# Eleven filter groups beside each image's scans in place of eight, and the stages ahead of them dealt more densely

## The chip, the cores and the metric

The kernel runs on one core of a Trainium2 chip. The metric is the device time of one execution in microseconds. Three runs of the kernel before took 11284.48, 11290.91 and 11290.32 us, a median of 11290.32. The profile is one further execution, of 11279.9 us.

## The reference

Four images of 64 x 64 positions with 128 channels pass through two layers, in 32-bit floats. What matters here:

```
# layer 0: four selective scans over 4096 positions (by rows, by columns, and both backwards),
# 256 channels, 16 states each
h = exp(dt * A) * h + (dt * u) * B          # one step per position
y = sum over the states of h * C
x = x + out_proj(norm(sum of the four y) * silu(z))
# then a mixture of 64 experts: softmax over positions, the top 8 of each expert,
# two matrices with a gelu between, scattered back and added to x
# layer 1: three matrices over x and its row and column sums, added to x, then on t = norm(x):
U_plus, U_minus = convolution of t with 16 long filters (4096 taps), plain and with alternating signs
out = sum over filters of U_plus @ Mpp[k] + U_minus @ Mpm[k]     # and three short taps
x = x + out
```

The long convolutions are computed as a block transform: positions go to 64 slots of a short Fourier transform, short filters are applied there, and the result is turned back.

## The kernel before, in words

**The scans.** The four images are worked on one after the other. An image's scans are four directions of eight chunks of 512 positions, 32 chunks, and each chunk has 16 steps, one for each state, 2048 steps in all. Both halves of 256 channels (128 partitions each) are in one step:

- SP loads the step's B and C, broadcast over partitions (`bc`), five steps ahead.
- ACT takes the exponential `da` (L1365), three steps ahead.
- DVE multiplies `db = du * B` (L1392, 128x1024) and runs two scans (L1398, 128x512) into `hh`, which has five buffers.
- POOL keeps the last state (L1407) and multiplies by C (L1408), one step later.
- PE sums over states by transposing `hh` into `y` (L1434), two steps later.

For every next chunk the step sizes are made meanwhile, a piece for each step: PE projects them (`dt_ps`, L1280), ACT and POOL make a softplus of them (`dl`, `dx`, L1282 to L1299), and ACT copies `dx` to PSUM as `du` at the chunk's end (`into_psum`, L1346), once the last `db` has been read.

**The work beside the scans.** Everything else is written as Python generators that issue a piece of work and yield its weight. `beside(b)` strings them together for the image whose scans are running: beside the first image the stages ahead of the other images' scans, beside image b the stages behind the scans of image b - 1. These are `after_scans` (the four `y` of an image are read back as `yk`, summed, normalised, gated and projected, L485 to L575), `experts_and_sums` (norms, logits, softmax, top 8, the two expert matrices `w1t` and `w2t` of 16 MB each, and layer 1's matrices) and `to_slots` (the transform, `fu_ps`, L1052). Then come groups of filters, `convolve`. Image 3's slot also turns image 0's results back (`from_slots`, `gi_ps`), and the first of these slots has one more gate.

`deal` is called twice in a step. It adds a share of the slot's total to what is due, and takes pieces until what has been made reaches it:

```
share["due"] += WEIGHT[chunks[i][0]] / ((K * NSC - FIRST) * (N - len(BUSY)) * 2)
while share["made"] < share["due"]:
    share["made"] += next(share["pieces"], 1e9)
    tick()
```

It deals nothing in an image's first chunk nor at the second and third step of any chunk. Each dealt instruction is pinned behind the scan's last instruction on its engine, and the next transpose of `y` behind the last dealt matmul, so the order on PE is the written one. Whatever is left at an image's end is run at once.

**A group of filters.** There are 64, sixteen an image, each over four slots of the transform. A group has four parts, in which 16 matmuls `cv_ps` (L1116) apply short filters and are evicted to `y` (L240, L238), and two accumulations of 16 matmuls `zq_ps` (L1137) with the matrices `me` and `mo`; the sum is transposed (`zt_ps`) and stored. Beside the scans a `cv_ps` pair weighs 4.0, a `zq_ps` matmul 2.0 and an eviction of `zq_ps` 4.0. There, PSUM leaves a single two-bank slot for `cv_ps`, `zq_ps` and the scans' own `dt_ps`. The trace counts two records for one of these 32-bit matmuls; transposes have one.

**The tail.** The groups that no scan covers follow the last scan, with eight banks of PSUM, evictions shared by ACT and DVE, and weights 4.0 for a `zq_ps` and 0 for `cv_ps`. A first loop runs the last image's three stages and deals filters between its pieces: for each unit of stage, `ratio` units of filters. A second one does the same with the turning back of images 1 and 2 and the last sixteen groups. At last image 3 is turned back.

Of the kernel before, what the change touches and what calls it, by code (L numbers as in the profile page):

```python
# [1 line left out]

# [1 line left out]

# [14 lines left out]
B, H, W, C = 4, 64, 64, 128  # L19
# [12 lines left out]


FIRST = 1
WEIGHT = (1346.0, 2087.0, 2005.0, 2059.0)

BUSY = (2, 3)

LAG = 5.0

BESIDE = 8


BS = 32
# [34 lines left out]
def kernel(  # L79
# [138 lines left out]
    def bank(shape, name):  # L218

        if side["ones"]:  # L220
            return side["ones"].tile(shape, F32, name=name, tag="ps")
        n = int(np.prod(shape[1:]))
        ap = pair(name)[0 : shape[0], 0, 0:n]
        if len(shape) == 2:
            return ap
        sizes = {f"d{i}": d for i, d in enumerate(shape[1:])}
        names = " ".join(sizes)
        return ap.rearrange(f"p ({names}) -> p {names}", **sizes)
# [5 lines left out]
    def evict(dst, src):  # L234

        side["n"] = side.get("n", 0) + 1
        if side["tail"] and side["n"] % 2:
            nc.vector.tensor_copy(dst, src)  # L238
        else:
            nc.scalar.copy(dst, src)  # L240
# [21 lines left out]
    def pipelined(n, *stages):  # L262


        for step in range(n + len(stages) - 1):
            for s in reversed(range(len(stages))):
                if 0 <= step - s < n and stages[s]:
                    stages[s][1](step - s)
                    yield stages[s][0]
# [49 lines left out]
    def sigmoid_of(pool, ps, h):  # L319


        n = ps.shape[-1]
        e = pool.tile([P, n], F32, name="sg_e")
        v = pool.tile([P, n], F32, name="sg_v", bufs=3)
        if h is None:
            nc.scalar.activation(e, ps, AF.Exp, scale=-1.0)
            nc.scalar.copy(v, ps)
        else:
            nc.scalar.activation(e, ps, AF.Exp, scale=-1.0, bias=ncb[:, h : h + 1])
            nc.scalar.activation(v, ps, AF.Identity, bias=cb[:, h : h + 1])  # L330
        nc.scalar.activation(e, e, AF.Ln, bias=1.0)
        nc.scalar.activation(e, e, AF.Exp, scale=-1.0)
        return v, e
# [121 lines left out]
    def gate(b):  # L455

        z_d[b] = dram.tile([2, P, L], F32, name=f"z_d{b}")
        with tc.tile_pool(name="pa_z", bufs=2) as pz:
            xn, vs = {}, {}

            def load(i):
                if i % 2 == 0:
                    g = i // 2
                    xn[g] = pz.tile([P, 512], F32, name="xn_z", bufs=4)
                    nc.sync.dma_start(xn[g], xn_d[b][:, 512 * g : 512 * (g + 1)])

            def project(i):
                g, h = divmod(i, 2)
                ps = bank([P, 512], "zp")
                nc.tensor.matmul(  # L470
                    ps, w_in_t[:, DI + h * P : DI + (h + 1) * P], xn[g], start=True, stop=True
                )
                vs[i] = sigmoid_of(pz, ps, None)

            def mul(i):
                v, s = vs[i]
                nc.gpsimd.tensor_mul(v, v, s)

            def put(i):
                g, h = divmod(i, 2)  # L480
                nc.sync.dma_start(z_d[b][h, :, 512 * g : 512 * (g + 1)], vs[i][0])

            yield from pipelined(16, (0.5, load), None, None, (2.8, project), (1.3, mul), (0.5, put))
# [551 lines left out]
    def to_slots(b):  # L1035

        with tc.tile_pool(name="fu", bufs=3) as fp:
            ub, uo = {}, {}

            def load(g):  # L1040

                ub[g] = fp.tile([NB, 4, 2, C], F32, name="ub")
                nc.sync.dma_start(
                    ub[g].rearrange("j t a c -> j (t a) c"),
                    u_d[b].rearrange("(j t) c -> j t c", j=NB)[:, 8 * g : 8 * g + 8, :],
                )

            def turn(g):
                uo[g] = fp.tile([P, 4, 2, C], F32, name="uo")
                for a in range(2):  # L1050
                    ps = bank([P, 4, C], "fu_ps")
                    nc.tensor.matmul(ps, fu_t, ub[g][:, :, a, :], start=True, stop=True)  # L1052
                    evict(uo[g][:, :, a, :], ps)

            def put(g):
                for r in range(2):
                    nc.sync.dma_start(
                        ud[b][:, r, 4 * g : 4 * g + 4], uo[g][r * NQ : (r + 1) * NQ]
                    )

            yield from pipelined(BS // 4, (0.5, load), (2.0, turn), (1.0, put))
# [122 lines left out]
    def from_slots(b):  # L1184

        with tc.tile_pool(name="gi", bufs=3) as gp:
            zb, xr, iv = {}, {}, {}

            def here(g):
                t0 = 2 * (BS - 4 * (g + 1))  # L1190
                return slice(t0, t0 + 8)

            def load(g):
                zb[g] = gp.tile([P, 4, 2, C], F32, name="zb")
                for r in range(2):
                    nc.sync.dma_start(
                        zb[g][r * NQ : (r + 1) * NQ], zd[b][:, r, 4 * g : 4 * g + 4]
                    )

            def turn(g):  # L1200
                xr[g] = gp.tile([NB, 4, 2, C], F32, name="xr3", bufs=4)
                nc.sync.dma_start(
                    xr[g].rearrange("j t a c -> j (t a) c"),
                    x3_d[b].rearrange("(j t) c -> j t c", j=NB)[:, here(g), :],
                )
                iv[g] = gp.tile([NB, 4, 2, C], F32, name="iv")
                for a in range(2):
                    ps = bank([NB, 4, C], "gi_ps")
                    nc.tensor.matmul(ps, gi_t, zb[g][:, :, a, :], start=True, stop=True)  # L1209
                    nc.scalar.activation(iv[g][:, :, a, :], ps, AF.Identity, scale=wpj[0:NB, :])  # L1210

            def add(g):

                for t in range(4):
                    nc.gpsimd.tensor_add(xr[g][:, t], xr[g][:, t], iv[g][:, 3 - t])  # L1215

            def put(g):
                nc.sync.dma_start(
                    out[b].rearrange("(j t) c -> j t c", j=NB)[:, here(g), :],
                    xr[g].rearrange("j t a c -> j (t a) c"),  # L1220
                )

            yield from pipelined(BS // 4, (0.7, load), (2.5, turn), (3.0, add), (0.5, put))
# [6 lines left out]
    all_groups = [(b, G) for b in range(B) for G in range(NQ // 4)]  # L1230

    def beside(b):

        if b == 0:
            for i in range(1, B):
                yield from before_scans(i)
            for i in range(B - 1):
                yield from gate(i)
            yield from filters()
        else:  # L1240
            yield from after_scans(b - 1)
            yield from experts_and_sums(b - 1)
            yield from to_slots(b - 1)
            if b == 1:
                yield from gate(B - 1)
            if b == B - 1:
                yield from from_slots(0)
            yield from convolve(all_groups[BESIDE * (b - 1) : BESIDE * b])

    with ExitStack() as c0:  # L1250
# [65 lines left out]
        def deal(*behind):  # L1316
# [4 lines left out]
            start = len(traced)  # L1321
            share["due"] += WEIGHT[chunks[i][0]] / ((K * NSC - FIRST) * (N - len(BUSY)) * 2)
            while share["made"] < share["due"]:
# [24 lines left out]
        for s in range(-5, total + 2):  # L1348
# [23 lines left out]
            if 0 <= s < total:  # L1372
                b, k, step, _ = chunks[i]
# [29 lines left out]
            if 0 <= t < total:  # L1403
                _, tk, tstep, _ = chunks[t // N]
                if tstep < NSC - 1:
                    last = 0 if tk >= 2 else SC - 1
# [63 lines left out]
    def first_stages():  # L1470
        yield from after_scans(B - 1)
        yield from experts_and_sums(B - 1)
        yield from to_slots(B - 1)
# [5 lines left out]
    last = len(all_groups) - NQ // 4  # L1479
    with tc.tile_pool(name="cv_tail", bufs=2) as cp:  # L1480

        for stages, groups, ratio in (
            (first_stages(), all_groups[BESIDE * (B - 1) : last], 3.2),
            (back(), all_groups[last:], 18.0),
        ):
            filtered = convolve(groups, cp)
            due = made = 0.0
            start = len(traced)
            for weight in stages:
                tick()  # L1490
                behind(start, False)
                start = len(traced)
                due += weight * ratio
                while made < due:
                    made += next(filtered, 1e9)
                    tick()
                behind(start, True)
                start = len(traced)
            run(filtered)
            behind(start, True)  # L1500
# [76 lines left out]
```

## Time and profile before

| | |
|---|---|
| median of three runs | 11290.32 us |
| the profiled execution | 11279.9 us |
| its span | 11278.1 us |
| scans of images 0, 1, 2, 3 start at | 301, 2437, 4633, 6876 us |
| last scan ends, first tail loop ends | 9088, about 10490 us |
| busy over the span: PE, DVE, ACT, POOL | 75%, 72%, 55%, 64% |
| POOL `hh` (L1408), one | 2359 ns, 2048 of them |
| DVE scan (L1398) and `db` (L1392), one | 1267 and 1232 ns |
| granted TensorE clock: scans of image 1, tail | 0.80, 0.99 to 0.98 |

A group's row has the line, engine, operation, and output from inputs, then its busy time, the mean of one, and the idle time just before it with what ended it. In the table by stretch each engine has its busy time and instructions in that stretch, then the granted clock, the share of time in which the DMA engines were busy, and GB/s. A row of waits names who waited for whom, the total in us, the number of waits and the longest. "Slot" below means the time of one image's scans; chunks are counted from 0 within it.

### The profile page before, as it was taken

What the parts mean: (1) busy time and instruction counts of PE and PEld (TensorE: products, weight loads), DVE (VectorE), ACT (ScalarE), POOL (GpSimd) and SP (SyncE); (2) the same over time, 40 slices, a digit from 0 to 9 for tenths busy, and PEclk for the clock granted to TensorE, in tenths of its full rate; (3) what the DMA queues carried; (4) which work ended last, traced back from release to release, by engine and by line L of the source; (5) the groups of instructions that cost most, each with busy time, mean ns of one, the idle gap of its engine ahead of it and who ended that gap; (6) DMA issues with size and microseconds to landing.
All of it is one profiled execution on the core that took longest, in us unless ns stands there. A gap on an engine that the chain in (4) does not pass through costs nothing. (4 is left out here: it accounts for less than half of the span.)

```text
span 11278.1 us, 117105 instructions
## 1 busy us (share of the span) xinstructions
PE 8435.7 (75%) x34656; PEld 4819.2 (43%) x34656; DVE 8146.8 (72%) x7046; ACT 6181.0 (55%) x12043; POOL 7262.7 (64%) x6518
## 2 busy tenths in 40 slices
PE   6677676556776777757766777576677789999998
PEld 2444443334453444444543344455344444355443
DVE  0898888887987999879878898798698932222222
ACT  4757575657466565664655566657455544124222
POOL 1888787888787877787867788888687821001001
PEclk9687787757777888878778788787788899999999
DMA  2565656566655666657565566575666664553555
GB/s 97 164 202 186 203 170 202 192 188 201 226 178 178 197 180 193 204 163 249 166 174 167 167 192 207 167 264 155 171 198 181 183 163 122 151 137 95 140 131 120
DMA packets 901457, 1980.14 MB, mean 176 GB/s; under 512 B 101562, under 2 KB 415578, under 8 KB 899290
## 3 DMA queue, kind: packets, MB, share of 16 engines
q1 hardware_dynamic: 900826, 1972.65, 58.2%
q8 instruction: 283, 4.64, 0.2%
q14 instruction: 348, 2.85, 0.1%
HBM read 1766.77 MB, written 205.52 MB: 175 GB/s over the span
## 5 line engine op out<-in xcount | busy, mean ns | idle before, releaser
L1408 POOL TENSOR_TENSOR hh<-hh,bc 128x1024 f32<-128x1024 f32 x2048 | 4829.8, 2359 | 434.2 <-DVE hh L1398 192.2
L1398 DVE TENSOR_TENSOR_SCAN hh<-da,hst,db 128x512 f32<-128x512 f32 x3584 | 4392.9, 1267 | 675.6 <-PE y L1434 297.9
L1365 ACT ACTIVATE da<-dl,aneg 128x512 f32<-128x512 f32 x4096 | 2766.3, 716 | 2084.4 <-DVE hh L1398 1998.3
L1434 PE MATMUL y<-ident,hh 128*128 128x128 f32 x16384 | 2808.2, 322 | 1214.8 <-POOL hh L1408 1095.7
L1434 PEld LDWEIGHTS y<-ident,hh 128*128 128x128 f32 x16384 | 2293.9, 167 | 2637.0 <-POOL hh L1408 1424.9
L1392 DVE TENSOR_TENSOR db<-du,bc 128x1024 f32<-128x1024 f32 x2048 | 2523.5, 1232 | 633.6 <-ACT du L1346 547.7
L1116 PE MATMUL cv_ps<-slab,us 64*128 64x512 f32 x4096 | 1197.3, 691 | 533.5 <-ACT y L240 277.8
L240 ACT COPY y<-cv_ps 128x512 f32<-128x512 f32 (+1 forms) x1024 | 754.3, 741 | 667.8 <-PE cv_ps L1116 638.0
L1407 POOL COPY hst<-hh 128x2 f32<-128x2 f32 x1792 | 338.9, 189 | 1123.6 <-DVE hh L1398 980.0
L1137 PE MATMUL zq_ps<-y,me 128*128 128x512 f32 x2048 | 1000.1, 609 | 49.0 <-ACT y L240 43.3
L1137 PE MATMUL zq_ps<-y,mo 128*128 128x512 f32 x2048 | 969.3, 597 | 0.0
L238 DVE COPY y<-cv_ps 128x512 f32<-128x512 f32 x640 | 441.5, 691 | 561.9 <-PE cv_ps L1116 511.8
L1116 PEld LDWEIGHTS cv_ps<-slab,us 64*128 64x128 f32 x4096 | 407.7, 206 | 1002.5 <-ACT y L240 369.3
L1153 POOL TENSOR_TENSOR zt<-zt,zt 128x512 f32<-128x512 f32 x64 | 81.2, 1268 | 996.2 <-DVE zt L238 536.5
L1398 DVE TENSOR_TENSOR_SCAN hh<-da,db 128x512 f32<-128x512 f32 x512 | 597.1, 1208 | 113.4 <-PE y L1434 70.8
L388 PE MATMUL cv_ps<-xh,diag 128*128 128x512 f32 x1152 | 534.7, 607 | 0.3 <-ACT xh L381 0.2
L1137 PEld LDWEIGHTS zq_ps<-y,me 128*128 128x128 f32 x2048 | 352.5, 193 | 382.2 <-issue 262.1
L1280 PE MATMUL dt_ps<-dts,dtw 8*128 8x512 f32 x512 | 371.4, 822 | 175.5 <-ACT dl L1283 48.3
L1137 PEld LDWEIGHTS zq_ps<-y,mo 128*128 128x128 f32 x2048 | 356.3, 191 | 316.6 <-issue 313.9
L1292 POOL TENSOR_TENSOR ex<-ex,dx 128x1024 f32<-128x1024 f32 x128 | 302.6, 2364 | 169.2 <-ACT dx L1289 169.0
L238 DVE COPY zt<-zq_ps 128x512 f32<-128x512 f32 x39 | 26.9, 691 | 529.0 <-PE zq_ps L1137 523.3
L510 PE MATMUL yk_ps<-yk,ident 128*128 128x512 f32 x512 | 275.2, 677 | 85.3 <-DMA yk<-y_d 34.0
(222 smaller groups left out, 8705.0 us busy)
## 6 DMA issues: line engine op xcount, KB each, us to landing
bc<-bc_d SPq DMA_DIRECT2D x2048, 512.0 KB
slab<-hd SPq DMA_DIRECT2D x1024, 256.0 KB
xc<-xc_d SPq DMA_DIRECT2D x128, 512.0 KB
y_d<-ys SPq DMA_DIRECT2D x128, 512.0 KB
w1t<-in_w_dram SPq DMA_DIRECT2D x128, 512.0 KB
w2t<-in_w_dram SPq DMA_DIRECT2D x256, 256.0 KB
xc_x<-xc_d SPq DMA_DIRECT2D x64, 512.0 KB
yk<-y_d SPq DMA_DIRECT2D x128, 256.0 KB
```

The costliest lines, as they stand in the source:

```text
L238: nc.vector.tensor_copy(dst, src)
L240: nc.scalar.copy(dst, src)
L388: nc.tensor.matmul(ps, diag[:, h, t, :], xh[:, 8 * g + dy : 8 * g + dy + 8, dx : dx + W], start=(t == 0), stop=(t == 8),)
L1116: nc.tensor.matmul(pq[q].rearrange("p (r k t) -> p r k t", r=2, t=BS), us[b, G][rows, p, a if e == 0 else 1 - a, :], slab[i][rows, p, :, : ...
L1137: nc.tensor.matmul(z, (me, mo)[e][:, KQ * kq + k, :], ys[e][:, :, :, :, k, :].rearrange("p a q r t -> p (a q r) t"), start=(e == 0 and k = ...
L1280: nc.tensor.matmul(ps, dtw[:, k, h * P : (h + 1) * P], dts, start=True, stop=True)
L1365: i_act = nc.scalar.activation(das[t][:, h, :], sizes[t // N][0][:, h, :], AF.Exp, scale=aneg[:, tk, h, t % N : t % N + 1],)
L1392: nc.vector.tensor_mul(db, dus[i], bcs[s][:, 0:1, :].to_broadcast([P, 2, SC]))
L1398: i_dve = nc.vector.tensor_tensor_scan(o, d0, d1, init, ALU.mult, ALU.add)
L1407: nc.gpsimd.tensor_copy(hsts[t // N][:, :, t % N], hhs[t][:, :, last])
L1408: i_pool = nc.gpsimd.tensor_mul(hhs[t], hhs[t], bcs.pop(t)[:, 1:2, :].to_broadcast([P, 2, SC]))
L1434: i_pe = nc.tensor.matmul(ys[c][:, q, h, :], hhs[t][:, h, q * P : (q + 1) * P], ident, is_transpose=True, start=(n == 0 and k > 0 and q % ...
```

## The change

Three of 64 filter groups more go beside each of the last three images' scans: the first of these slots takes groups 0 to 10, the second 11 to 21, the third 22 to 32. Nine groups fewer are left to the first tail loop (15 in place of 24), whose ratio of filters to stages falls from 3.2 to 2.0. In `beside`, the pieces of the stages ahead of the filters are the same, in the same order, but each counts with 0.65 of its weight, so that 1/0.65 = 1.54 times as many are dealt in a step. Filters keep their weights, and the slots' totals are set to the new sums. The first image's slot is untouched, and so are the second tail loop and all operations themselves.

```diff
-WEIGHT = (1346.0, 2087.0, 2005.0, 2059.0)
+WEIGHT = (1346.0, 2128.0, 2075.0, 2110.0)
...
-BESIDE = 8
+BESIDE = 11
+
+CLOSER = 0.65
...
-            yield from after_scans(b - 1)
-            yield from experts_and_sums(b - 1)
-            yield from to_slots(b - 1)
+            front = [after_scans(b - 1), experts_and_sums(b - 1), to_slots(b - 1)]
             if b == 1:
-                yield from gate(B - 1)
+                front.append(gate(B - 1))
             if b == B - 1:
-                yield from from_slots(0)
+                front.append(from_slots(0))
+            for weight in chain(*front):
+                yield CLOSER * weight
             yield from convolve(all_groups[BESIDE * (b - 1) : BESIDE * b])
...
-            (first_stages(), all_groups[BESIDE * (B - 1) : last], 3.2),
+            (first_stages(), all_groups[BESIDE * (B - 1) : last], 2.0),
```

## The prediction

> **What bounds the kernel now.** I read first the page's slices, to see the regimes.
>
> ```profile
> ## 2 busy tenths in 40 slices
> PE   6677676556776777757766777576677789999998
> DVE  0898888887987999879878898798698932222222
> POOL 1888787888787877787867788888687821001001
> PEclk9687787757777888878778788787788899999999
> ```
>
> In the first thirty-two slices (about 282 us each) DVE leads: the scans. In the last eight PE is alone at 9: the tail. So the kernel has two bounds, and the change moves work across the border. Next, the busy time by stretch, cut where the scans of each image start (301, 2437, 4633, 6876), where they end (9088), and where the first tail loop ends (10490); below it one bare chunk, and the slot of image 1 (the first with filters) cut into its stages.
>
> ```profile
> core 0: us, PE busy (x) PEld busy (x) DVE busy (x) ACT busy (x) POOL busy (x), PEclk, DMA share, GB/s
> 2437.00:4633.00 2196.00, 1555.97 (x7169) 968.91 (x7168) 1903.84 (x1561) 1349.08 (x2557) 1740.72 (x1507) 0.80 0.62 193
> 9088.00:10280.00 1192.00, 1151.62 (x4030) 523.07 (x4030) 289.41 (x413) 411.93 (x1106) 142.26 (x339) 0.99 0.54 136
> ...
> 4633.00:4692.00 59.00, 33.68 (x157) 26.98 (x155) 56.41 (x48) 29.64 (x44) 48.72 (x37) 0.59 0.50 164
> ...
> 2501.00:2727.00 226.00, 158.82 (x760) 107.80 (x760) 176.60 (x144) 164.56 (x388) 194.38 (x235) 0.84 0.77 231
> 2727.00:2896.00 169.00, 93.00 (x436) 72.56 (x436) 131.30 (x112) 115.32 (x310) 119.29 (x131) 0.65 0.38 128
> 2896.00:3212.00 316.00, 245.80 (x1363) 161.12 (x1364) 293.18 (x242) 153.69 (x229) 254.36 (x175) 0.86 0.75 260
> 3212.00:3624.00 412.00, 256.76 (x1295) 183.44 (x1293) 306.26 (x249) 280.19 (x726) 323.78 (x381) 0.74 0.54 164
> 3624.00:4121.00 497.00, 378.38 (x1564) 204.28 (x1564) 469.35 (x385) 302.30 (x431) 398.92 (x276) 0.85 0.65 192
> ```
>
> An image's scans are 32 chunks of 16 steps. The row 4633:4692 is one chunk with nearly nothing beside it: its base is PE 34, ACT 30, POOL 49 us, DVE filling 56 of 59. In 3624:4121, eight chunks with filters beside them, a chunk takes 62.1 us and DVE is 94% busy: filters are nearly free there. The stages before them take chunks 1 to 15: 1123 us in this slot, 1113 in each of the next two, 74 us a chunk. Not all alike: chunks 6 to 10 (the experts, 2896:3212) take 63 us each, the ten others about 80. Who holds DVE up in 2501 to 3624:
>
> ```profile
> DVE hh L1398 <- PE y L1434: 84.2, 21, 16.6
> DVE db L1392 <- ACT du L1346: 38.0, 6, 11.0
> ```
>
> The scan's output buffer is freed by PE's transposes, which stand behind stage matmuls, and the next chunk's du is an ACT copy behind stage work. So stages cost scan time, filters hardly any. Last, PE's groups of the first tail loop (9088 to 10490) and its longest wait there:
>
> ```profile
> L1116 PE MATMUL cv_ps<-slab,us 64*128 64x512 f32 x1521 | 374.4, 613 | 21.8 <-ACT y L240 15.3 <-DVE y L238 3.4 <-DMA slab<-hd 2.5
> L1137 PE MATMUL zq_ps<-y,me 128*128 128x512 f32 x752 | 357.4, 605 | 3.6 <-ACT y L240 3.6
> L1137 PE MATMUL zq_ps<-y,mo 128*128 128x512 f32 x752 | 348.6, 599 | 0.0
> ...
> PE cv_ps L1116 <- ACT y L240: 15.3, 17, 2.4
> ```
>
> All PE waits of these 1402 us sum to 47 us: here each filter group costs its full PE time.
>
> **What the skill says.** "TensorE: Matmul & The Clock Gate", on the array's architecture, says that PE keeps matmuls in program order and pulls only weight loads ahead, and that ACT and DVE are strict first-in-first-out. The waits agree: a late stage matmul or ACT operation shows up as a stopped scan (84.2 and 38.0 us). Its part on the HAM clock gate says that an idle PE is clocked down; 0.80 in the scans against 0.99 in the tail agrees in direction. "DMA: Bandwidth & Descriptors", "Issuing engines are not separate DMA queues": all transfers interleave on the same 16 engines. In the chunk in which the scan outputs are read back the share reaches 0.93 against 0.50 in a bare one. "Perfetto Trace Analysis", "Optimization Strategy": a bubble that repeats can mean too little PSUM. It does here, at the third term below.
>
> **The change, term by term.** *Units.* A slot deals its weights evenly over 31 chunks. A group of filters weighs 64 + 60 + 8 = 132 beside the scans, so the three slots' stages weigh 2087, 2005 and 2059 less 8 x 132 + 10, that is 1021, 939 and 993. At 67.3, 64.7 and 66.4 a chunk they take 15.2, 14.5 and 15.0 chunks. Afterwards a chunk deals 68.6, 66.9 and 68.1, and a stage unit counts 0.65: 9.7, 9.1 and 9.5 chunks. Eleven groups with their 1462 units fill the rest; 0.65 x 1021 + 1462 = 2126 against 2128, so nothing is left to run in one burst at the end. Filters remain at 1.97 chunks a group (1.99 before). The issue order of the changed program bears this out: filters begin in chunk 10 in place of 15 or 16. In the tail 24 groups become 15: 128 units a group and 10, over the ratio, gives 963 stage units before and 965 after, so filters and stages still end together. The number of instructions, and of bytes moved, is the same; the transfers of a stage (loads of yk, weights, x) move with it, in SP's queue beside the bc loads.
>
> *Tail: -396 + 30.* A group's PE time: 374 + 357 + 349 + 14 for zt, 1094 us over 24 groups is 45.6; in the pure stretch later 14 groups with 27 us of other matmuls take 625 us, 42.7 each. I take 44: nine are 396 us. What it costs: the cover of the stages' latencies falls from 24 x 44 to 15 x 44 beside some 300 us of stage matmuls. A piece that buys 3.2 units of filters now buys 2.0, so each lead shrinks by over a third before its filler; next to be late are yk (7.4 us waited already) and ub (4.7 us). At 47 us of waits now, I add 30; ends 0 and 100. The second loop is unchanged.
>
> *Stages in the scans: +171.* Experts: beyond the base of five chunks they use 246 - 170 = 76 us of PE and 0.75 x 316 - 150 = 87 us of DMA share. In 3.2 chunks that is 58 and 57 us a chunk, just under 62. I take 66: 3.2 x 66 + 1.8 x 63 - 311 = +14 a slot. The ten others: POOL is busy 194 + 119 + 324 = 637, 147 beyond its base; ACT 165 + 115 + 280 = 560, 260 beyond. In 6.4 chunks POOL needs 6.4 x 49 + 147 = 461, 72 a chunk, and ACT 452, 71 a chunk. Today the busier fills 64 of 80, 0.79. At 0.79 a chunk would take 91, and the slot would lose nothing: 6.4 x 91 + 3.6 x 63 = 809 against 805. But two engines would now be near their limit together, and DMA in the yk chunk: its 69 us of share (0.93 of 74.5) is 38 beyond the base, and 44 yk matmuls are issued in that chunk in place of 32, giving about 84. So I take 97: 6.4 x 97 + 3.6 x 63 - 805 = +43. Sum 57 a slot, 171 in three. Ends: -40 (fewer chunk ends, each with a wait for du) and +345 (ACT the limit everywhere: 25 us lost per removed chunk, five and a bit a slot, less what is shared).
>
> *Filters' phase: about 0.* Beside filters one PSUM slot serves cv, zq and dt_ps, so the next chunk's dt_ps must wait if zq is accumulating. Half a group is 66 units, almost one chunk, so the phase drifts slowly. In the second image's slot, chunks 16 to 23, dt_ps ran 39 to 45 us into the chunk, not 12 to 20; ACT then waited eight times, 55.9 us in all, for POOL's dl, and the chunks took 71.2 us, some 8 above 63: 62 us. In the changed order dt_ps stands late (half-steps 18 down to 10 of 32) in chunks 11 to 18 of the first slot and 13 to 10 in four of the third, never in the second. By the same 8 us, falling to 0 at half-step 10, that is 45 + 13. It cancels; ends -40 and +60.
>
> Sum: -396 + 30 + 171 - 4 = -199. The profiled execution took 11279.9 us, of which 11278.1 is the span: 11081. The median of runs lies 10 us above it: **11091 us**.
>
> **Rivals.** *Slower: the stages jam the scans.* Filler and stage matmuls block y in PE's order, dl on POOL is late, DVE stops. It decides where the ten chunks pass 107 us (POOL filled to 0.67): 6.4 x 107 + 227 - 805 = 107, with 14 times three just offsets the tail. At 116 us: 3 x (164 + 14) - 366 - 4 = +164, 11454. For it: some chunks run at 90 to 103 us already, with up to 42 us of wait for y. Against: those have short bursts (fu waiting for ub), and the experts run at the bare speed. 0.10. *Tail cover gone.* PE waits for yk, h1, the top-k and ub; the first tail loop takes some 1190 us rather than 1036: -45, 11245; from 11230 to 11313 I put 0.10, half within 0.2%. For it: serial chains over softmax, top-k and gelu; against: only 47 us of waits now. *Stages free.* The excess per unit stays: -396 + 30 = -366, 10924. For it: POOL at 0.79 would do; against: the yk chunk's DMA. 0.08. That the moved groups don't move is excluded by the issue order.
>
> **How the numbers follow.** The forecast (10970 to 11230) gets 0.72. Adding about half of the free-stage case and the nearer part of the tail case makes 0.8: 10955 to 11265. By sign, with 0.2% (23 us), about what a measurement here can tell from none: faster 0.72 + 0.08 + 0.05 = 0.85, same 0.05, slower 0.10.
>
> **What would show it.** The last y transpose ends near 9255 (9088 + 171 - 4), and the tail takes about 1825 us in place of 2190. Chunks 1 to 9 of slots 1 to 3 average 85 to 90 us, the experts' 66, filters' chunks 63, with waits of ACT for dl in slot 1, not 2. PE waits of the first tail loop sum to 60 to 100 us. Wrong if the last y comes after 9450, or if the tail shrinks by less than 250.

## The result, and the profile after

The changed kernel takes **11454.75 us**, median of four runs (11453.7 to 11459.15), against 11289.81 for the kernel before on the same chip: a ratio of 1.0149, 95% interval 1.0136 to 1.0161. It is slower by 165 us, which is 1.5% but far outside the spread of the runs, where the prediction had it faster by 199. The profiled execution's span is 11451.9 us against 11278.1, 173.8 us more. The starts and the end of the scans split that:

| stretch | before, us | after, us | difference | predicted |
|---|---|---|---|---|
| before the first scan | 301 | 300 | -1 | 0 |
| slot of image 0 | 2136 | 2139 | +3 | 0 |
| slots of images 1, 2, 3 | 2196, 2243, 2212 | 2459, 2318, 2406 | +263, +75, +193 | +167 in all |
| tail | 2190 | 1830 | -360 | -366 |

The tail came out as predicted to 6 us. The three slots became longer by 531 us and not by 167. The page's slices of the kernel after:

```profile
## 2 busy tenths in 40 slices
PE   6777676545766677766777777667677777999998
...
DVE  0898888875757889976779999776588996212222
...
POOL 1888788876766777776768877766677775202001
PEclk9687787667868888877778888777788888999999
```

Three dents are new in the row of DVE, in slices 9 to 13, 18 to 21 and 26 to 29: the first part of each slot, the dense stages. PE isn't near 9 there, it is at 4 to 7, and POOL is down at 6 and 7. No engine is busier than before where more work per step was dealt. The table by stretch, with the columns as before (a time, then each engine's busy time, clock, DMA share, GB/s): the slot of image 1, its chunks 1 to 10 (the stages) and its last eight chunks, in the kernel after,

```profile
core 0: us, PE busy (x) PEld busy (x) DVE busy (x) ACT busy (x) POOL busy (x), PEclk, DMA share, GB/s
2439.00:4898.00 2459.00, 1728.70 (x7561) 1017.25 (x7560) 1904.25 (x1561) 1403.91 (x2613) 1746.63 (x1510) 0.80 0.58 178
...
2503.00:3477.00 974.00, 653.77 (x3172) 430.10 (x3172) 613.48 (x505) 575.51 (x1438) 648.37 (x756) 0.75 0.57 183
...
4387.00:4898.00 511.00, 392.15 (x1595) 212.50 (x1594) 469.44 (x385) 301.91 (x429) 400.46 (x278) 0.84 0.63 186
```

and the same stages in the kernel before, chunks 1 to 15:

```profile
2501.00:3624.00 1123.00, 754.38 (x3852) 524.92 (x3852) 907.35 (x744) 713.77 (x1651) 891.81 (x919) 0.78 0.62 199
```

A third of the chunks is gone from this stretch, and only 149 us. Ten chunks take 97.4 us each; the busiest engine, PE, works in 67% of that time. The transfers aren't it either: their share fell from 0.62 to 0.57. Nor did the matmuls themselves get longer at the lower clock (0.75 after 0.78): the stages' `yk_ps` take 70.8 us before and 70.4 after, `h_ps` from `w2t` 68.6 and 65.4. The last eight chunks are as they were, 511 us against 512 (4121 to 4633) in the kernel before.

What fills the time shows in PE's waits. In the kernel before, in those 1123 us (who waited for whom, the total in us, the number, the longest):

```profile
PE y L1434 <- POOL hh L1408: 153.3, 61, 17.4
PE lg_ps L716 <- ACT tT L240: 33.6, 8, 9.1
PE fu_ps L1052 <- DMA ub<-u_d: 23.2, 3, 20.1
PE zp L470 <- ACT sg_v L327: 18.9, 8, 4.5
```

In the kernel after, in its 974 us:

```profile
PE xn_ps L319 <- ACT xn L307: 42.4, 29, 8.0
PE lg_ps L719 <- ACT tT L243: 34.3, 6, 10.2
PE yt_ps L532 <- ACT y L243: 31.9, 6, 12.5
PE pk_ps L775 <- POOL pT L765: 24.9, 2, 24.4
PE tt_ps L319 <- ACT tt L307: 19.2, 8, 17.6
PE cv_ps L1119 <- DMA slab<-hd: 19.1, 2, 18.8
```

Two kinds of waits have to be told apart. When a transpose of `y` waits for POOL's `hh`, PE is ahead of the scans: that time is PE's slack. When a stage matmul waits for its input from ACT, POOL or a load, PE is held, and the transposes of `y` behind it with it. I call these side waits. Sorted so, waits of the scans' own transposes apart:

| slot of image 1 | time | PE busy | slack | side waits |
|---|---|---|---|---|
| before, chunks 1 to 15 | 1123 | 754 | 173 | 191 |
| after, chunks 1 to 10 | 974 | 654 | 4 | 316 |

(A few microseconds belong to neither.) The other two slots read the same: slack 177 and 178 before, 11 and 10 after, side waits 177 and 176 before, 264 and 298 after. So PE, at 67% busy, has no free time: its order is full. The slack is used up, and the side waits grew, though there are fewer instructions in the stretch. By the engine that ended them, ACT's share rose from 113 to 205 us and POOL's from 21 to 62, while that of loads fell from 58 to 37. DVE sees the other end of it. Its waits in the same 974 us:

```profile
DVE hh L1401 <- PE y L1437: 165.1, 42, 19.6
DVE hh L1401 <- ACT da L1368: 28.8, 10, 10.8
DVE db L1395 <- ACT du L1349: 25.3, 4, 10.8
```

The first was 84.2 in the 1123 us before. The waits for `du`, which come once a chunk, fell from 38.0 as the chunks became fewer. The wait for `y` is 165 of 343 us that DVE waits in all, after 84 of 180: about half. In the other half DVE waits for ACT and POOL directly, or its own stage instructions do (50 us, 19 before), so PE's order isn't the only place in which the scans are held. The tail in the kernel after, PE's groups of the first loop, then its longest wait there:

```profile
L1119 PE MATMUL cv_ps<-slab,us 64*128 64x512 f32 x930 | 246.2, 634 | 18.4 <-ACT y L243 11.1 <-DVE y L241 3.8 <-DMA slab<-hd 3.1
L1140 PE MATMUL zq_ps<-y,me 128*128 128x512 f32 x464 | 224.4, 610 | 1.2 <-ACT y L243 1.2
L1140 PE MATMUL zq_ps<-y,mo 128*128 128x512 f32 x464 | 220.9, 604 | 0.0
...
PE cv_ps L1119 <- ACT y L243: 11.1, 8, 2.7
```

The loop takes 1039 us (9621 to 10660) in place of 1402, PE idle for 54 of them, against 45 before. The thinner cover was nearly free: PE's busy time there fell by 372 us.

### The profile page after: what moved, and what is told of

Read it like the earlier page. It is cut to its first block, busy times and chain, and to the rows that moved or that the text cites. A ratio compares the mean times of both kernels' runs of the same rounds, so it can differ in the third digit from the quotient of the medians.

```text
span 11451.9 us, 116853 instructions
## 1 busy us (share of the span) xinstructions
PE 8539.8 (75%) x34656; PEld 4809.2 (42%) x34656; DVE 8038.2 (70%) x6888; ACT 6249.9 (55%) x12056; POOL 7264.9 (63%) x6518
## 5 line engine op out<-in xcount | busy, mean ns | idle before, releaser
L1401 DVE TENSOR_TENSOR_SCAN hh<-da,hst,db 128x512 f32<-128x512 f32 x3584 | 4393.1, 1267 | 1205.5 <-PE y L1437 591.1
L1395 DVE TENSOR_TENSOR db<-du,bc 128x1024 f32<-128x1024 f32 x2048 | 2523.3, 1232 | 540.8 <-ACT du L1349 460.6
L1119 PE MATMUL cv_ps<-slab,us 64*128 64x512 f32 x4096 | 1283.7, 722 | 650.7 <-ACT y L243 422.9
L243 ACT COPY y<-cv_ps 128x1024 f32<-128x1024 f32 (+1 forms) x1024 | 814.7, 800 | 736.5 <-PE cv_ps L1119 702.1
L241 DVE COPY y<-cv_ps 128x512 f32<-128x512 f32 x496 | 341.6, 691 | 495.6 <-PE cv_ps L1119 464.6
L1218 POOL TENSOR_TENSOR xr<-xr,iv 64x256 f32<-64x256 f32 x128 | 88.4, 718 | 412.5 <-ACT iv L1213 377.9
```

The source lines that it names most:

```text
L1119: nc.tensor.matmul(pq[q].rearrange("p (r k t) -> p r k t", r=2, t=BS), us[b, G][rows, p, a if e == 0 else 1 - a, :], slab[i][rows, p, :, : ...
L1395: nc.vector.tensor_mul(db, dus[i], bcs[s][:, 0:1, :].to_broadcast([P, 2, SC]))
L1401: i_dve = nc.vector.tensor_tensor_scan(o, d0, d1, init, ALU.mult, ALU.add)
```

## The experiments

| run | us | ratio to before (95%) | last scan ends |
|---|---|---|---|
| before | 11290 | | 9088 |
| the change | 11455 | 1.0149 (1.0136 to 1.0161) | 9621 |
| dense8 | 11767 | 1.0425 (1.0404 to 1.0446) | 9578 |
| eleven_loose | 11683 | 1.0350 (1.0333 to 1.0367) | 9847 |
| leads | 11423 | 1.0120 (1.0100 to 1.0140) | 9596 |
| own_bank | 12260 | 1.0862 (1.0840 to 1.0884) | 10407 |
| lighter_pe, lighter_act | 11346, 11242 | one run each | 9600, 9434 |
| phase | 11320 | 1.0027 (1.0019 to 1.0036) | 9479 |
| da6 | 11478 | 1.0170 (1.0151 to 1.0188) | 9640 |
| hh6 | 11319 | 1.0028 (1.0016 to 1.0041) | 9487 |
| phase_hh6 | 11177 | 0.9903 (0.9887 to 0.9920) | 9336 |
| before_hh6 | 11221 | 0.9938 (0.9924 to 0.9953) | 9029 |
| nine | 11248 | 0.9962 (0.9949 to 0.9976) | 9196 |
| nine_phase | 11216 | 0.9941 (0.9927 to 0.9954) | 9146 |
| ten_phase | 11242 | 0.9963 (0.9951 to 0.9976) | 9301 |
| ten_phase_hh6 | 11159 | 0.9884 (0.9869 to 0.9898) | 9218 |
| nine_phase_hh6 | 11132 | 0.9860 (0.9845 to 0.9874) | 9076 |

**Which part of the change costs.** The change has two parts, denser stages and more groups behind them. The first run keeps the density and takes the groups back:

```diff
-BESIDE = 11
+BESIDE = 8
...
-            (first_stages(), all_groups[BESIDE * (B - 1) : last], 2.0),
+            (first_stages(), all_groups[BESIDE * (B - 1) : last], 3.2),
```

> The denser stages alone: eight groups a slot, with the same weights and slot totals as in the change, so that stages and the first eight groups are dealt as densely as there and the last chunks of a slot have nothing beside them; the tail is that of before (24 groups, ratio 3.2). If the density of the stages is what costs, the last scan ends about where it does in the change, near 9600 us, and with the 2190 us of the old tail the time is some 11790 us. If the three more groups beside the scans cost scan time of their own, the scans end earlier by that, and the time is below 11700.

The row of its stages in the slot of image 1, and of its tail:

```profile
2502.00:3475.00 973.00, 655.54 (x3172) 432.42 (x3172) 614.19 (x506) 576.48 (x1440) 650.22 (x756) 0.75 0.57 183
...
9578.00:11767.00 2189.00, 2110.48 (x7103) 941.70 (x7101) 541.22 (x780) 688.70 (x1625) 260.66 (x532) 0.99 0.53 132
```

The stages take 973 us as in the kernel after, though nothing follows them but the old eight groups at their old weights. Of the 533 us by which the scans end later, 490 are there without a single moved group; the nine groups themselves add 44 (9621 less 9578). The first of the two outcomes written down came. The price is in the stages' density, the late step sizes that it brings included (see below).

The second run does the opposite: stages as dense as before, and the eleven groups packed 1.37 times as densely into the chunks behind them.

```diff
-WEIGHT = (1346.0, 2128.0, 2075.0, 2110.0)
+WEIGHT = (1346.0, 2864.0, 2751.0, 2825.0)
...
-CLOSER = 0.65
+CLOSER = 1.3715
```

> Eleven groups a slot, but the stages dealt exactly as densely as before (67, 65 and 66 units a chunk), and instead the filters 1.37 times as densely. If the density of the stages is the cost and filters are nearly free, the stages' chunks go back to 74 us, filters' chunks stay at 62 to 65, and the gain of the tail of 360 us is kept: 10930 us, with up to 100 more for filters' chunks. If it is the larger amount of work beside the scans, wherever it stands, that costs, the time stays near that of the change, above 11350.

The stages' chunks are back at 62 to 96 us in the slot of image 1, but the filters' chunks, 62 to 65 before, take 70 to 93, and the time is 229 us above the change's. PE's waits in the kernel before, in its chunks 17 to 30 of image 1 (3687 to 4571), where DVE is 93% busy:

```profile
PE cv_ps L1116 <- ACT y L240: 75.2, 46, 6.3
PE y L1434 <- POOL hh L1408: 46.4, 12, 6.6
PE cv_ps L1116 <- ACT zt L240: 38.1, 11, 6.2
```

In those 884 us PE is busy for 680 and slack is 46: its order was 95% full before the change. In the run with denser filters, over chunks 17 to 30 (3700 to 4874), a table row and the waits:

```profile
3700.00:4874.00 1174.00, 860.26 (x3147) 429.84 (x3148) 823.96 (x674) 580.73 (x808) 708.42 (x499) 0.83 0.52 153
...
PE cv_ps L1119 <- ACT y L243: 151.3, 104, 5.4
PE zq_ps L1140 <- ACT y L243: 42.3, 17, 2.9
```

Of 1174 us, 860 are busy and nearly all the rest side waits; waits of `y` for the scans come to some 2 us. DVE waits for `y` for 237 us there, in the kernel before for 20. So filters at the old density only seemed nearly free: they filled PE's order to the brim, with DVE as the other limit. At these densities there was no room for three more groups in either place.

**What the side waits are made of.** Three runs change the kernel after inside the stages. In the first, the chains get more room: an empty step of the pipeline between producer and consumer, more buffers for it, the stages' pauses (`LAG`) at their full weight, and loads of `z` and `xr` moved nearer to their use, with fewer buffers.

```diff
-                z[g] = po.tile([P, 2, 256], F32, name="z", bufs=5)
+                norm_apply(y[g], y[g], st[g], 2)
+
+            def load_z(g):
+                z[g] = po.tile([P, 2, 256], F32, name="z", bufs=4)
...
+                    None,
...
-                yield CLOSER * weight
+                yield weight if weight == LAG else CLOSER * weight
```

> The change, with longer leads at nearly the same density: one more empty step in the stages' pipelines between an operation and the one on another engine that uses it, with the buffers that this takes, and the pauses (LAG) at their full weight; two loads of after_scans are issued a few steps nearer to their use, because memory lacks room. If the cost is that instructions of the stages come to the head of their engine's queue before their input is there, well over half of the 466 us of the stages goes: 11200 us or less. If it is that ACT, POOL and DMA are too full in the dense stretch, nothing changes by more than 60 us: 11390 to 11510.

It gains 32 us. Side waits fall from 316 to 257 in the slot of image 1, but only by 15 and 33 in the other two. Its chunks 1 to 10 of image 1:

```profile
2506.00:3432.00 926.00, 651.85 (x3172) 431.52 (x3172) 613.79 (x506) 574.74 (x1436) 651.85 (x756) 0.77 0.59 191
```

With as many matmuls as in the kernel after, these ten chunks are 48 us shorter, and 23 in each of the other slots: 94 in all. Most of that is lost again behind them, where chunks 11 to 31 take 66 us more. There the filters start at another moment, and the step sizes are late in more chunks (half-steps 16 to 10 in six chunks of the first slot, 10 in three of the second, 18 to 10 in eight of the third; what that means follows below). So longer leads bring back part of the stages' loss, more than the 32 us show; how much they would be worth with good step sizes wasn't run.

In the next, PE has less to do. Two of the four `yk` are summed, half of the experts' matmuls are done and one of three taps, so the output isn't the reference's:

```diff
-                    for e in range(EG):
+                    for e in range(1):
...
-                            for i in range(3):
+                            for i in range(1):
```

> The change with less PE work in the stages, and everything else as it was: after_scans sums two of the four scans' outputs in place of four, each expert loop uses one expert of every two, and the regression takes one of three taps; all loads, evictions, ACT and POOL operations stay. By the tail's durations that is 31 + 30 + 31 + 16 = 108 us of PE a slot. If PE's queue is what holds the scans up in the dense stages, the last scan ends 200 to 330 us earlier than in the change (9621), at 9290 to 9420, and the tail shortens by about 100. If ACT or POOL hold it up and PE merely waits for them, the last scan ends within 80 us of the change.

```profile
2500.00:3457.00 957.00, 576.88 (x2660) 380.10 (x2660) 613.62 (x505) 575.35 (x1438) 647.94 (x756) 0.71 0.58 186
```

77 us of matmuls are gone from these ten chunks, and 17 us of time: side waits rose from 316 to 370. The scans end 22 us earlier, within the 80 that had been written down for this case. PE waits for its inputs; what it computes isn't the load.

In the third, ACT has less: the sums of the norms are taken over every second tile only, and the output again isn't the reference's.

```diff
+        n //= 2
...
-                bias=nm[:, q : q + 1],
-                scale=r[:, q : q + 1],
+                bias=nm[:, q // 2 : q // 2 + 1],
+                scale=r[:, q // 2 : q // 2 + 1],
```

> The change with less ACT work in the stages: the sums of every norm are taken over every second tile only, and used for its neighbour too; PE, POOL and loads stay as they were. That is some 57 us of ACT a slot. If PE waits for stage inputs because ACT has too much to do, the last scan ends 120 to 250 us earlier than in the change (9621). If PE's own matmuls are the load and ACT is only late by the leads, it ends less than 80 us earlier.

```profile
2460.00:3371.00 911.00, 643.31 (x3172) 426.82 (x3172) 611.80 (x505) 528.10 (x1181) 646.07 (x756) 0.77 0.61 195
```

ACT's busy time falls by 47 us (575 to 528), the time by 63, the side waits by 59 (to 257); those that ACT ends fall from 205 to 114, as few as before the change. The scans end 187 us earlier, some 24 of it before the first scan and 17 in the slot of image 0. In chunks 1 to 10 of the three slots, 139 us less of ACT's work come with 154 us less of time. So ACT's work in front of a stage matmul counts about one to one, at an ACT that is 59% busy: it is a latency in a chain, not a full engine. In its own order, ACT stands still for `da`, which waits for DVE's scan to free a buffer (481 us over the stages of the three slots). I took that for a closed loop: scan, `da`, stage output, stage matmul, `y`, scan. If it were the loop's tightest point, one more buffer of `da` would loosen it.

```diff
-            dl = pb.tile([P, 2, SC], F32, name="dl", bufs=3)
+            dl = pb.tile([P, 2, SC], F32, name="dl", bufs=2)
...
-                das[t] = pb.tile([P, 2, SC], F32, name="da", bufs=5)
+                das[t] = pb.tile([P, 2, SC], F32, name="da", bufs=6)
```

> The kernel after with six buffers of da in place of five (and two of dl in place of three, for the space). If the stage chunks are long because ACT's da waits for the scan to free a buffer while the stage outputs that PE waits for stand behind da in ACT's order, one buffer more lets ACT run a step further ahead and the last scan ends over 80 us earlier than the 9621 of after. If the stage chunks are long only because each PE wait is a latency between PE and ACT that is paid anyway, the scans end within 40 us of 9621; then the waits of ACT for the scans are a consequence of the stopped scans, not their cause.

It gains nothing (last scan at 9640, ratio 1.0170 against 1.0149). ACT's waits for the scans are a result of the stopped scans. (The space came from the third buffer of `dl`, here and in the next run. That loss wasn't run alone, but in neither trace did ACT wait before it wrote `dl`.) The buffer at the other end of the loop is a different matter:

```diff
-            dl = pb.tile([P, 2, SC], F32, name="dl", bufs=3)
+            dl = pb.tile([P, 2, SC], F32, name="dl", bufs=2)
...
-                hhs[s] = pb.tile([P, 2, SC], F32, name="hh", bufs=5)
+                hhs[s] = pb.tile([P, 2, SC], F32, name="hh", bufs=6)
```

> The kernel after with six buffers of the scan's output hh in place of five (and two of dl in place of three). The scans stop in the stages because y stands in PE's order behind blocked stage matmuls, and y frees hh. If the blocks are bursts, one step more of slack (about 1.9 us of DVE) is bought at each of them and the last scan ends over 80 us earlier than 9621. If PE's queue is full on average in these chunks, a deeper buffer only shifts the moment at which DVE stops, and the scans end within 40 us of 9621.

The time falls by 135 us, the scans end 134 earlier. (One more buffer is worth a whole step of DVE, which is 3.8 us by 1232 and two times 1267 ns, not the 1.9 of the expectation.) DVE's waits over the whole span, in the kernel after,

```profile
DVE hh L1401 <- PE y L1437: 629.6, 196, 19.6
...
DVE hh L1401 <- ACT da L1368: 79.2, 40, 10.8
```

and with six buffers:

```profile
DVE hh L1401 <- PE y L1437: 415.8, 115, 19.5
DVE hh L1401 <- ACT da L1368: 140.1, 47, 10.1
```

214 us less for `y` and 61 more for `da`; the waits for `du` rise by 71 (460.6 to 531.6), and a number of smaller ones make up the rest. The chunks tell where: chunks 1 to 10 gain 26, 25 and nothing, and chunks 11 to 31 gain 86 in all. So each of the two readings seems to hold in its place. In the filters' chunks PE is blocked in bursts, and a buffer bridges them; in the dense stages its order is full on average, and a buffer buys little (26 us of 974).

**The late step sizes.** `deal` is called twice in a step, so a chunk has 32 half-steps, and beside filters `dt_ps` usually stands in one of the first six. In the issue order of the kernel after it stands at half-steps 18 to 10 in eight chunks of the first slot and 13 to 10 in four of the third, behind the filters that share its one PSUM slot. One run splits PSUM beside the filters into one bank for `dt_ps` and one for `cv_ps` and `zq_ps`:

```diff
-            slots(0, 1)
+            slots(1, 0, 1)
...
+                            if not side["tail"]:
+                                evict(to[:, q], pq[q])
+                                yield 2.0
```

> The change, with the two-bank PSUM slot beside filters split into one bank for the projection of the step sizes and one for filters, whose matmuls are then evicted one bank at a time. If the late step sizes behind an open accumulation are why filters' chunks take 66 to 68 us in the slots of images 1 and 3, these fall to 62 to 64 and the time by 100 to 150 us, to 11300 to 11350. If these chunks are long for another reason, the time stays within 40 us of the change, or is longer by the smaller evictions.

It can't decide that, for it slows the filters down in another way. The groups of `cv_ps` in eight chunks of filters (image 1's last), first of the kernel after, then of this run:

```profile
L1119 PE MATMUL cv_ps<-slab,us 64*128 64x512 f32 x256 | 96.7, 816 | 76.6 <-ACT y L243 42.1 <-ACT zt L243 19.8 <-ACT dl L1286 9.9
```

```profile
L1122 PE MATMUL cv_ps<-slab,us 64*128 64x512 f32 x256 | 226.0, 977 | 42.0 <-ACT y L243 25.2 <-ACT zt L243 11.4 <-DVE db L1401 2.8
```

256 records of 816 ns are 209 us, in 96.7 us of busy time: the two matmuls of a pair, one on partitions 0 to 63 and one on 64 to 127, run at once. (A group has 16 such pairs, 32 matmuls `cv_ps`.) With one bank the second has to wait for the eviction of the first (250 us of records in 226). The Trainium skill has the ground of it, in "TensorEngine Tiling (Array Packing)", "Overview": the array can work as several smaller independent ones. PE's busy time in these chunks rises from 392 to 553 us and the stretch from 511 to 605. The run shows again that PE's order is full here.

The other way is to leave PSUM alone and shift the filters' start, by dealing the stages a little closer, so that `dt_ps` hardly ever stands later than half-step 8:

```diff
-CLOSER = 0.65
+CLOSER = (1.0, 0.615, 0.65, 0.626)
...
-                yield CLOSER * weight
+                yield CLOSER[b] * weight
```

(with totals of 2092, 2075 and 2085.)

> The change with the first and third of its slots' stages dealt slightly more densely still (0.615 and 0.626 in place of 0.65), so that the filters begin some ten and seven half-steps earlier and the projection of the step sizes never stands later than half-step 8. If late step sizes are why filters' chunks cost 66 to 68 us there, chunks 11 to 20 of image 1's slot fall from 71 to 64 us and chunks 11 to 16 of image 3's likewise, and the time falls by 80 to 110 us, less some 10 to 20 for the denser stages: 11350 to 11390. If these chunks are long for another reason, they stay at 70 us and the time is at 11455 or above.

It gains 135 us, more than the 65 to 105 that were expected, with denser stages than the change itself. Slots of 2459, 2318 and 2406 us become 2369, 2318 and 2357: the two with late step sizes gain 90 and 49, the one without gains nothing. ACT's waits in the first slot, from the end of the stages (3477 to 4188) in the kernel after,

```profile
ACT da L1368 <- POOL dl L1300: 53.8, 9, 8.0
```

and from 3448 to 4145 in this run:

```profile
ACT da L1368 <- POOL dl L1300: 3.8, 1, 3.8
```

**Are these two losses or one, and are they the change's?** Both cures together, and the buffer in the kernel before:

> Eleven groups with step sizes never late (11320) and six buffers of hh, two of dl. The two cures together: if they are for different losses (late step sizes in the filters' chunks, full queue in the stages), the gains of 135 us each add to some 250 and it takes 11180 to 11220. If the sixth buffer only covers late step sizes, it takes 11290 to 11320, and the density of the stages, some 300 us against before, is left whole.

> The kernel before with six buffers of hh and two of dl. If the gain of 135 us that this gave to the kernel after (11320) is the price of the change's density, that is of blocks that a chunk without slack can't make up, the kernel before, whose PE still waits 173 us for the scans in a slot's stages, gains clearly less: 11220 to 11270. If the sixth buffer is a gain of its own, whatever the density, it is 11130 to 11180, and the change costs the same with it.

Together they gain 277 us (11177), as much as both apart: two losses. The kernel before gains 69 from the sixth buffer (11221). Its DVE waits over the whole span, before,

```profile
DVE db L1392 <- ACT du L1346: 547.7, 50, 289.5
...
DVE hh L1398 <- PE y L1434: 368.7, 115, 17.5
```

and with six buffers:

```profile
DVE db L1392 <- ACT du L1346: 636.0, 59, 288.9
...
DVE hh L1398 <- PE y L1434: 221.0, 43, 14.4
```

148 us less, and 88 of them come back as waits for `du` at the chunk's end: net 60, and the scans end 59 earlier. So half of the buffer's gain in the kernel after was there before the change, and half came with it. That half isn't due to late step sizes: in the run without them, the buffer is worth 143 us (11320 to 11177). The late step sizes aren't the change's alone either: the kernel before has them in eight chunks of its second slot, and their cure wasn't run there.

**How many groups.** Nine groups with stages at 0.866 of their weight and a ratio of 2.8; then nine with stages at 0.866, 0.92, 0.866 and ten at 0.73, 0.75, 0.75, so that no step sizes are late; then both with six buffers:

```diff
-BESIDE = 11
+BESIDE = 9
...
-CLOSER = 0.65
+CLOSER = (1.0, 0.866, 0.92, 0.866)
```

> A small step in the direction of the change: nine groups a slot, filters as dense as before, stages 1/0.866 = 1.15 times as dense. If PE's queue is full already before the change, a group costs about as much of it beside the scans as it saves in the tail, and the time lies within 40 us of before, 11250 to 11330. If the cost comes only beyond some density between, the gain of the tail (3 groups, 130 us) is kept for the most part: 11160 to 11220.

> Nine groups beside each image's scans, stages at 0.866, 0.92 and 0.866 of their weight in the three slots, so that no dt_ps stands later than half-step 5 in a chunk of filters (but one at 8 or 9 in each slot's first). The run with nine groups and 0.866 throughout had dt_ps at half-steps 15 to 19 in seven chunks of the second slot, which took some 8 to 10 us more each: without them the last scan should end near 9135 rather than 9196, the tail stays at some 2050, and the time is 11170 to 11210, about 0.99 of before. If the late step sizes were not what made those chunks long, the time is 11235 to 11260 as with nine groups at 0.866.

> Ten groups beside each image's scans, stages at 0.73, 0.75 and 0.75 of their weight, step sizes never late in the filters' chunks. Each slot's density lies between nine groups (0.866) and eleven (0.615 to 0.65 with good step sizes: 11320). If the cost of density rises smoothly from the full PE queue, the tail gains another 130 us over nine groups and the scans lose some 160 to 190: 11190 to 11260. If there is a threshold, below which denser stages are free as the prediction had it, it should be as fast as 11100.

> Nine groups with step sizes never late (11216) and six buffers of hh, two of dl. Between before and after in density: if the sixth buffer pays where chunks have no slack, it gains 40 to 90 us: 11125 to 11175. If the gain in the kernel after was that of its late step sizes alone, which are absent here, it gains under 20.

> Ten groups with step sizes never late (11242) and six buffers of hh, two of dl. If the sixth buffer pays where chunks have no slack, it gains 60 to 110 us here, 11130 to 11180, and ten groups draw level with nine. If it pays for late step sizes alone, under 20.

From eight groups to nine, both with step sizes late in eight chunks of the second slot, the scans end 108 us later (9196 after 9088) for 134 us less of tail, and the time falls by 41 us, to 11248. With good step sizes the scans end at 9146, 9301 and 9479 us for nine, ten and eleven groups a slot: three more groups in all cost 155 and then 178. The tail takes 2056, 1939 and 1835, so they give 117 and then 104. With six buffers the scans lose 142 and 118 for 117 and 106. None of these steps was free, so no threshold shows between eight and eleven below which denser stages cost nothing. With good step sizes nine is the best number tried, each step towards eleven losing more than it gains; ten with six buffers doesn't draw level, as had been expected. Nine groups with good step sizes and six buffers beat both kernels: 11132 us, 0.9860 of before. Of that 157 us, 69 are what the buffer gives to the kernel before, and some are the cure of the late step sizes. Nine's 11248 and 11216 lie just outside the ranges written down, by 2 and 6 us. Eight groups with good step sizes weren't run.

## Why the prediction was wrong

**Right in sum: the tail.** "-396 + 30" is measured at -360. The first tail loop takes 363 us less: PE is busy for 372 us less, 41 a group and not 44, and idle for 9 us more and not 30. The direction of both terms was right, but the misses of 24 and 21 us cancel, which is luck.

**Wrong: "Stages in the scans: +171".** Chunks 1 to 10 take 974, 933 and 960 us, after 1123, 1113 and 1113 for chunks 1 to 15. Five chunks of filters at 63.2 take the place of the missing five, so the slots lose 167, 136 and 163: **+466**. (63.2 is the mean of filters' chunks with good step sizes in the kernel before.) The experts' step holds roughly (chunks 5 and 6, wholly inside it, take 64 to 75 us; 66 expected). The step that failed is "I take 97" for the other chunks. With the experts at some 70 us, the 6.4 chunks of the first slot took about 113, an estimate: (974 less 3.2 x 70 and 0.4 x 63) / 6.4. That is past the break-even of 107 and close to the 116 of the rival "the stages jam the scans". That rival had the mechanism; that the time met its 11454 is luck in part, since it has +534 for the stages and -4 for the filters' phase, where 466 and 66 were measured. The prediction's own sign of being wrong, a last `y` after 9450, came too (9625).

The reason is in the working of that step. It took the busier of POOL and ACT and filled it to 0.79, as before. POOL is filled to about 0.64 in these chunks (72 us of 113), below even the 0.67 at which the rival decides, so POOL's work isn't the limit. What the step didn't cost is the waiting in PE's order: 67% busy before (754 of 1123) looks like room, and with side waits it was 84% full. Had they stayed at 191, the ten chunks would have needed 654 + 191 = 845 us, about what was forecast (6.4 x 97 + 3.2 x 66 + 0.4 x 63 = 857). They grew to 316 instead. As I read it, each is a latency through ACT and POOL, and 1.54 times as many pieces a step leave less time between a piece and its consumer. Fewer matmuls didn't shorten them (lighter_pe), longer leads did in part, and less ACT work did about one to one. The prediction quoted the Trainium skill on PE's program order ("TensorE: Matmul & The Clock Gate", which has it in "Step-by-step: what each phase is for"), but read only DVE's side of it, 84.2 us of waits for `y`, and not PE's list, in which the largest entry, 153 us for the scans, was nearly all the slack there was (173).

**Wrong: "filters are nearly free", behind "Filters' phase: about 0".** The late step sizes were seen, and in the right chunks. Two sizes were off. In all three slots together the filters' chunks took 85 us more than 63.2 each before, and 151 more after: +66, not -4. Removing the late step sizes gave 139 us in the two slots against 58 forecast: 110 of it in the filters' chunks, the rest in the stages. "Falling to 0 at half-step 10" was wrong: chunks 18 to 20 of the first slot, at half-steps 10 to 8, still took 67 to 71 us. The waits of ACT for `dl` in the first slot were as forecast (53.8 us, 55.9 in the kernel before's bad chunks), but the chunks lost more than that. I take it that a filter chunk whose PE order is 95% full doesn't make up what it loses, and that the blocked matmuls come on top.

Terms measured: -360 + 466 + 66 is +172, and +173.8 was the span's. The misses are 6, 295 and 70 us.

Two slips in the working are small. Eleven groups at the new totals take 1.94 chunks each and not 1.97, so filters were dealt some 3% more densely as well; and the experts' five chunks are set at 311 us, where the table has 316.

The "0.10" for the stages' jam rested on chunks "at 90 to 103 us already" being "short bursts". They were the chunks with the most side waits: in chunks 4, 14 and 15 of the first slot of before (92, 98 and 86 us) these came to 40, 27 and 30 us, with 4 to 8 us of slack, while chunks 3, 5, 11, 12 and 13 had 0 to 15 us of side waits and 12 to 25 of slack. So the jam was there before, in a few chunks.

**Open.** Which of ACT's pieces holds which matmul wasn't separated further; the side waits are spread over a dozen pairs, none above 43 us. That they are longer because of the density itself is argued from the counts, and supported by lighter_act; a run with the stages' chains taken out of ACT's order wasn't made. Nor was one that loosens `da` and `hh` together, or the waits of DVE that aren't for `y`.

## What to carry to other kernels

Before work is dealt more densely on an in-order engine, split its idle time by who it waits for: only waits for the stream that must not stop are slack, and waits of the filler's own instructions count as occupied. An engine at 67% busy can be full, and these waits grow with the density, so the cost of a denser deal is not the busy time it adds. When a slot is at such a limit, look first for the buffer that lets the critical stream ride over a block, and for a phase that repeats chunk after chunk: here each was worth 135 us of the 165 that the change had cost, though the buffer gave 69 without the change too.

## What was not expected of the hardware

Two 64-row matmuls of a pair overlap almost wholly (209 us of records in 96.7), and with one PSUM bank the same 256 records take 226 us of PE, 0.5 us more for each record.
